# The edge stage of a four-layer graph network: a fixed order for ScalarE's copies and one-hots

## The chip, the cores and the metric

One core of one Trainium2 chip. The metric is the device time of one execution in microseconds; the median of three timed runs is shown. Besides it there is one profiled execution, whose trace gives every instruction's start and duration.

Names used below: TensorE (PE, matrix multiply; its weight loads are PEld), VectorE (DVE), ScalarE (ACT), GpSimd (POOL) and SyncE (SP, which here only issues transfers). Each engine runs its own instructions in a fixed order that is laid out when the program is built; between engines they wait for one another by semaphores. SBUF is the on-chip memory, PSUM the accumulator memory that TensorE writes, divided into banks.

## The reference, cut to what matters

Four graph layers over 3125 nodes of 128 features and 103125 edges, which are sorted by their target `dst`; each layer is followed by a residual addition and a layer norm. The stage in question works for all four: it turns the list of edges into dense matrices. The first layer is

```python
def _L0_gnn_ref(x, edge_row, edge_col, edge_val, weight, b):
    xw = x @ weight
    msgs = edge_val[:, None] * xw[edge_col]
    out = jax.ops.segment_sum(msgs, edge_row, num_segments=N_NODES)
    return jax.nn.relu(out + b)
...
edge_index = jnp.stack([src, dst])
x = _layernorm(x + _L0_gnn_ref(x, src, dst, edge_weight, L0_gnn_weight, L0_gnn_b), axis=-1)
x = _layernorm(x + _L1_gnn_ref(x, edge_index, ...), axis=-1)
x = _layernorm(x + _L2_gnn_ref(x, ...), axis=-1)
x = _layernorm(x + _L3_gnn_ref(x, edge_index, ...), axis=-1)
```

(with the weights' names shortened). The second and third layers are attentions over the same edges, the fourth takes means over them twice. The kernel replaces the gathers and segment sums by products with two dense 3125 x 3125 matrices: how often an edge from one node to another occurs (the counts), and the sum of those edges' weights (the weights). As several edges can share a pair of nodes, both are sums.

## The kernel before, in words

**The matrices.** The edge stage makes both matrices from one-hot vectors. A *window* takes five nodes (`WN` = 5) and up to 256 edge slots, which lie as two halves of 128 on the partitions. An edge's source node is written as a row d (0 to 127) within a block c (0 to 24). `ohd` holds, for each edge slot, the one-hot of d; `ohc` the one-hot of the pair (node of the window, block c), 125 of 128 columns (`KW` = 125). A product of the two over the edge slots gives the counts of a window. For the weights `ohd` is multiplied by the edge's weight first; to keep single precision, the weight is split into three bfloat16 parts, and so there are three such tensors, `wod[0]`, `wod[1]` and `wod[2]`.

**Batches and groups.** Sixteen windows (`BW` = 16) form a batch, four windows a group; there are 40 batches (`NBT`), the last with one group, 157 groups in all. For each batch `make(b)` (from line 827) has VectorE make `ohd` and `ohc` (line 849) and the `wod` (line 860): the first two for both halves, the third for the first half only. The second half of the third is made by ScalarE, window by window: `more(k)` (line 863) is four activations that scale one window's one-hot each (line 866). These sixteen per batch are the *one-hots on ScalarE* of this text. The pools `f_oh` (two buffers for each of `ohd`, `ohc`) and `f_of` (six for the `wod`) hold two batches, so the tensors of batch b+1 are made while TensorE works on batch b.

**One group.** For group k of batch b TensorE adds eight matmuls (line 893: four windows, two halves) into the bank `cp`, the counts, and 24 (line 901: four windows, two halves, three parts) into the bank `wp`, the weights. ScalarE then casts `cp` into `cs` in bfloat16 (line 906) and copies `wp` into `ws` (line 912). `cp` and `wp` come from one pool of three PSUM banks (`f_cps`, tag "cw"); the transposes for new keys (lines 675 and 676) use the same three. In the program's text, the four one-hots of the next batch's group k stand between the cast of `cs` and the copy of `ws` (lines 906 to 912).

**After a batch.** SyncE stores `ws` into the dense matrix `wd` (line 914) and, after every second batch, `cs` into the matrix of counts `ctd` (line 917). In the first two batches `xw_of` multiplies the features by the first layer's weights (lines 760 to 770). From the third batch on `add0` (line 801) begins the first layer's sum: for 128 finished rows of `wd` it loads two tiles `cw` of ten blocks each (line 807) and adds them into five banks that stay open, by fp32 matmuls (line 811); the trace counts 40 of them for 128 rows. Every eighth batch `keys_of` (lines 659 to 699) prepares the keys and weights of the next 128 windows, with six transposes on TensorE and copies on VectorE and ScalarE.

**What sets the order.** The text of the program gives each instruction its rank; the tool that builds the program goes through the engines with its own estimates of time and lets the first-ranked ready instruction of each engine go next. The order so found is fixed: on the chip each engine takes its instructions in it. `tc.issue_after(i)` adds an edge of order without a semaphore: what is traced inside stands after instruction i on i's engine. Before the change none is used for these copies and one-hots, so a one-hot may be put ahead of copies of its own and earlier groups as soon as `ohd` of its batch is made.

Of the kernel before, what the change touches and what calls it, by code (L numbers as in the profile page):

```python
# [10 lines left out]
AF = mybir.ActivationFunctionType  # L11
# [6 lines left out]
NB = 25  # L18
# [471 lines left out]
WN = 5  # L490
NW = 640
NG = 5
BW = 16
KW = WN * NB
# [16 lines left out]
def fast_path(  # L511
# [4 lines left out]
    nc = tc.nc  # L516
# [225 lines left out]
    def products_of_weights():  # L742
        nc.gpsimd.tensor_tensor(both, gb_row, sb_row, OP.add)
        tw = {}
        for name, w in (("l1", l1_wt), ("q", wqt), ("k", wkt), ("v", wvt)):
            t = zps.tile([P, P], F32, name="trw", tag="acc3")
            nc.tensor.transpose(t, w, ident)
            tw[name] = ep.tile([P, P], F32, name="tw_" + name)
            nc.scalar.copy(tw[name], t)
        t = zps.tile([P, P], F32, name="trw", tag="acc3")  # L750
        nc.tensor.matmul(t[:, 0 : 2 * H], tw["l1"], att, start=True, stop=True)
        nc.scalar.copy(watt, t[:, 0 : 2 * H])
        t = zps.tile([P, P], F32, name="trw", tag="acc3")
        nc.tensor.matmul(t, tw["q"], tw["k"], start=True, stop=True)
        nc.scalar.copy(wyv[:, 0:P], t)
        t = zps.tile([P, P], F32, name="trw", tag="acc3")
        nc.tensor.matmul(t, tw["v"], wot, start=True, stop=True)
        nc.scalar.copy(wyv[:, P:], t)

    def xw_of(b0, n):  # L760

        t = zps.tile([P, 512], F32, name="trx", tag="acc0")
        for k in range(n):
            nc.tensor.transpose(t[:, k * P : (k + 1) * P], x[:, b0 + k, :], ident)
        xT = ep.tile([P, 512], F32, name="f_xTb", bufs=2)
        nc.scalar.copy(xT[:, : n * P], t[:, : n * P])
        t = zps.tile([P, 512], F32, name="trx", tag="acc2")
        for k in range(n):
            nc.tensor.matmul(t[:, k * P : (k + 1) * P], xT[:, k * P : (k + 1) * P], l0_wt, start=True, stop=True)
        nc.scalar.copy(xw[:, b0 : b0 + n, :].rearrange("p b d -> p (b d)"), t[:, : n * P])  # L770
# [26 lines left out]
    def bias0(acc, n):  # L797
        for j in range(n):
            nc.tensor.matmul(acc[:, j, :], ones, l0_br, start=(j == 0), stop=False, skip_group_check=True)

    def add0(pool, i, accs, blocks):

        b0, n = blocks
        for h in range(0, n, 10):
            m = min(10, n - h)
            cw = pool.tile([P, min(10, n), P], F32, name="cw")[:, 0:m]
            nc.sync.dma_start(
                cw.rearrange("p c d -> p (c d)"), wd[i * P : (i + 1) * P, (b0 + h) * P : (b0 + h + m) * P]
            )
            for j in range(h, h + m):  # L810
                nc.tensor.matmul(  # L811
                    accs[j // 4][:, j % 4, :], cw[:, j - h, :], xw[:, i, :], start=False,
                    stop=(i == NB - 1 and (j % 4 == 3 or j == n - 1)), skip_group_check=True,
                )
# [12 lines left out]
    def make(b):  # L827

        if b % 8 == 2 and 8 < b < NBT - 8:
            keys[b // 8 + 1] = keys_of(b // 8 + 1)  # L830
        kd2, kc2, w2, w3 = keys[b // 8]
        ohd = op_.tile([P, 2 * BW, P], BF16, name="ohd")
        ohc = op_.tile([P, 2 * BW, P], BF16, name="ohc")

        def twos(k):
            k = k[:, b % 8, :, :, :].rearrange("p q w t -> p (q w) t")
            return k[:, :, None, :].to_broadcast([P, 2 * BW, P // 2, 2])

        def some(s):
            if b < NBT - 1:  # L840
                return [slice(0, 2 * BW if s < 2 else BW)]
            return [slice(0, LW)] + ([slice(BW, BW + LW)] if s < 2 else [])

        def packed(o, ww):
            return o[:, ww].rearrange("p w (a t) -> p w a t", t=2)

        for o, k in ((ohd, kd2), (ohc, kc2)):
            for ww in some(0):
                nc.vector.tensor_tensor(  # L849
                    packed(o, ww), twos(k)[:, ww],  # L850
                    ramp.rearrange("p (a t) -> p a t", t=2)[:, None, :, :].to_broadcast(
                        [P, ww.stop - ww.start, P // 2, 2]
                    ),
                    OP.is_equal,
                )
        wod = []
        for s in range(3):
            f = of_.tile([P, 2 * BW, P], BF16, name="wod")
            for ww in some(s):
                tip[s] = nc.vector.tensor_tensor(packed(f, ww), packed(ohd, ww), twos(w2[s])[:, ww], OP.mult)  # L860
            wod.append(f)

        def more(k):
            for w in range(k, k + 4):
                at = (b % 8) * BW + w
                nc.scalar.activation(wod[2][:, BW + w, :], ohd[:, BW + w, :], AF.Copy, scale=w3[:, 1, at : at + 1])  # L866

        return ohd, ohc, wod, more

    cs = None  # L870
    acc0 = None
    done = 0
    cur = make(0)
    with tc.issue_after(tip[0].ins), tc.issue_after(tip["keys"].ins):
        keys[1] = keys_of(1)
# [2 lines left out]
    for b in range(NBT):  # L878
        ohd, ohc, wod, _ = cur
        cur = make(b + 1) if b + 1 < NBT else None  # L880
        nw = BW if b < NBT - 1 else LW
        if b % SB == 0:
            cs = sp.tile([P, NB, SB * BW * WN], BF16, name="cs")
            if b + SB == NBT:
                nc.gpsimd.memset(cs[:, :, ((SB - 1) * BW + LW) * WN :], 0.0)
        ws = sp.tile([P, BW, P], F32, name="ws")
        for k in range(0, nw, 4):
            cp = cps.tile([P, 4, P], F32, name="cp", tag="cw")
            wp = cps.tile([P, 4, P], F32, name="wp", tag="cw")
            for j in range(4):  # L890
                for q in range(2):
                    w = q * BW + k + j
                    nc.tensor.matmul(  # L893
                        cp[:, j, 0:KW], ohd[:, w, :], ohc[:, w, 0:KW], start=(j == 0 and q == 0), stop=(j == 3 and q == 1),
                        skip_group_check=True,
                    )
            for j in range(4):
                for q in range(2):
                    w = q * BW + k + j
                    for s in range(3):  # L900
                        made = nc.tensor.matmul(  # L901
                            wp[:, j, :], ohc[:, w, :], wod[s][:, w, :], start=(j == 0 and q == 0 and s == 0),
                            stop=(j == 3 and q == 1 and s == 2), skip_group_check=True,
                        )
            i0 = (b % SB) * BW * WN + k * WN
            nc.scalar.copy(  # L906
                cs[:, :, i0 : i0 + 4 * WN].rearrange("p c (w i) -> p c w i", i=WN),
                cp[:, :, 0:KW].rearrange("p w (i c) -> p c w i", c=NB),
            )
            if cur and (b + 1 < NBT - 1 or k < LW):  # L910
                cur[3](k)
            nc.scalar.copy(ws[:, k : k + 4, :], wp)  # L912
        for a, e in ((0, 112), (112, KW)):
            nc.sync.dma_start(wv_[b * BW : b * BW + nw, a:e, :].rearrange("w k d -> k w d"), ws[a:e, 0:nw, :])
        if b % SB == SB - 1:
            i0 = (b - SB + 1) * BW * WN
            nc.sync.dma_start(ctd[:, :, i0 : i0 + SB * BW * WN].rearrange("c d i -> d c i"), cs)
        if b < 2:
            for blocks in GB[4 * b : 4 * b + 4]:
                xw_of(*blocks)  # L920
        if b == 2:
            with tc.issue_after(made.ins):
                products_of_weights()
            acc0 = [zps.tile([P, 4, P], F32, name=f"acc{k}", tag=f"acc{k}") for k in range(Z0 // 4)]
            for a in acc0:
                bias0(a, 4)
        while acc0 and (done + 1) * P <= (b - 1) * BW * WN:
            add0(zp, done, acc0, (0, Z0))
            done += 1
# [150 lines left out]
    with ExitStack() as st:  # L1080
# [119 lines left out]
        cp = st.enter_context(tc.tile_pool(name="f_cp1", bufs=6))  # L1200
# [120 lines left out]
        for x_, (g, hp, c) in enumerate(items):  # L1321
            i0, n = IG[g]
# [49 lines left out]
    scale = float(P) ** -0.5  # L1372
    with ExitStack() as st:
        l2 = st.enter_context(tc.tile_pool(name="f_lp2", bufs=1))
        yT = l2.tile([P, NP], F32, name="yT")
        cp = st.enter_context(tc.tile_pool(name="f_cp2", bufs=3))
# [79 lines left out]
        for x_, (q, c) in enumerate(items):  # L1456
            i0, n = QG[q]
# [40 lines left out]
    with ExitStack() as st:  # L1498
        fp = st.enter_context(tc.tile_pool(name="f_fp3", bufs=1))
        cp = st.enter_context(tc.tile_pool(name="f_cp3", bufs=HB + 1))  # L1500
# [77 lines left out]
        for k in range(K + 3):  # L1578
            if k < K:
                for b in range(NB - HB, NB):  # L1580
                    add1(last[b], b, k)
                c, n = CN[k]
# [172 lines left out]
```

## Time and profile before

| what | value |
|---|---|
| median of three timed runs | 1514.52 us (1514.36 to 1517.14) |
| the profiled execution: time | 1519.3 us |
| its span, first to last instruction | 1517.5 us |
| busy share of PE / PEld / DVE / ACT over the span | 92% / 80% / 65% / 60% |
| mean granted TensorE clock | 0.983 |
| first cast of `cs`, end of the last copy of `ws` | 47.2 us, 469.2 us |

The costliest rows of the edge stage by the page's list of groups:

| line, engine | what | times | mean ns of one | busy us |
|---|---|---|---|---|
| 901 PE | wp, 24 per group | 3768 | 219 | 239.1 |
| 893 PE | cp, 8 per group | 1256 | 218 | 95.7 |
| 811 PE | first layer's sum | 1000 | 278 | 118.7 |
| 860 DVE | wod | 122 | 1870 | 221.2 |
| 866 ACT | one-hots | 628 | 399 | 192.8 |
| 912 ACT | copy of ws | 157 | 584 | 91.7 |

The mean of a matmul is its whole passage; matmuls overlap, so a group's busy time is far below count times mean, and the pace of TensorE is read from starts. The same holds for ScalarE and VectorE to a lesser degree (a one-hot of 395 ns follows another after some 295 ns). In the timeline a line gives start, duration, engine, line, and in brackets the idle time before it and what ended it; "x12" means that twelve instructions of one kind stood in a row. Of the 1000 matmuls of line 811, 160 belong to rows and blocks that are done after the edge stage.

### The profile page before, as it was taken

The page shows a single profiled execution, that of the slowest core. Times are in us where ns is not written, and L with a number is a line of the kernel's source. Part 1 is how long each engine was busy: PE and PEld are TensorE (multiplying, and loading weights), DVE is VectorE, ACT ScalarE, POOL GpSimd, SP SyncE. Part 2 cuts the span into 40 slices and gives each one's busy share as a digit, 9 for nine tenths or more (in the row PEclk, how much of TensorE's full clock was granted, in tenths as well). Part 3 has the DMA queues.
Part 4 walks back from the last instruction along what each step waited for, and adds up shares of the span by engine and source line. Part 5 has one row for each costly group of instructions (what it writes and reads, how often), then busy time and mean ns, then how long its engine had stood idle before and what let it go on. Part 6 is the DMA issues. An engine that isn't in the chain of part 4 may idle for free.

```text
span 1517.5 us, 35041 instructions
## 1 busy us (share of the span) xinstructions
PE 1390.6 (92%) x14775; PEld 1218.8 (80%) x14775; DVE 982.5 (65%) x1621; ACT 906.6 (60%) x1847; POOL 129.5 (9%) x164
## 2 busy tenths in 40 slices
PE   4898999999998988988979989899999999999995
PEld 3898999899897888987978979677777774458995
DVE  4999998989991389887898879534465352012006
ACT  2988888878882479877867788454555331023003
POOL 1000000000000022231132113200000000000000
PEclk9999999999999999999999999999999999999998
DMA  7368787877889644443433434332222218513541
GB/s 204 92 177 235 209 225 188 242 197 210 234 225 261 200 131 119 112 130 112 135 95 105 143 89 116 117 118 73 69 60 80 73 59 303 195 44 130 197 154 46
DMA packets 209734, 223.92 MB, mean 148 GB/s; under 512 B 72988, under 2 KB 183371, under 8 KB 209309
## 3 DMA queue, kind: packets, MB, share of 16 engines
q1 hardware_dynamic: 208780, 218.51, 49.6%
q8 instruction: 117, 1.92, 0.5%
q0 software_dynamic: 400, 1.97, 0.4%
q10 hardware_dynamic: 385, 1.11, 0.2%
q14 instruction: 52, 0.43, 0.1%
HBM read 157.19 MB, written 64.36 MB: 146 GB/s over the span
## 4 chain that ended last, share of the span: by engine, by line
PE 71%; ACT 12%; DVE 9%; DMA 3%; issue 3%; POOL 2%; SPq 0%; ACTq 0%; DVEq 0%; POOLq 0%
PE acc L1272 9%; PE acc L1423 9%; PE wp L901 8%; PE s L1415 8%; PE acc L811 7%; PE acc L1523 7%; PE acc L1599 6%; ACT wod L866 5%; PE acc L1267 5%; DVE cm L1257 3%; PE cp L893 3%; PE left L811 2%; ACT ws L912 2%; DMA cw<-wd 1%; DVE cm L1250 1%
## 5 line engine op out<-in xcount | busy, mean ns | idle before, releaser
L1272 PE MATMUL acc<-vp,cm 128*128 128x198 bf16 x2500 | 343.4, 251 | 7.6 <-DVE cm L1257 6.6
L1267 PE MATMUL acc<-vp,ct 128*128 128x204 bf16 x1250 | 317.0, 255 | 9.7 <-DVE vp L1175 4.5
L1256 ACT ACTIVATE fm<-adr,bas 128x768 bf16<-128x768 f32 (+1 forms) x320 | 287.1, 952 | 62.3 <-DVE cm L1257 60.5
L1272 PEld LDWEIGHTS <-cm 128*128 128x128 bf16 x2500 | 235.8, 98 | 24.5 <-DVE cm L1257 8.9
L901 PE MATMUL wp<-wod,ohc 128*128 128x128 bf16 x3768 | 239.1, 219 | 5.6 <-ACT cs L906 5.6
L901 PEld LDWEIGHTS <-ohc 128*128 128x128 bf16 x3768 | 219.9, 98 | 6.7 <-issue 6.3
L860 DVE TENSOR_TENSOR wod<-ohd,w 128x4096 bf16<-128x4096 bf16 (+2 forms) x122 | 221.2, 1870 | 0.6 <-PE wp L901 0.6
L1257 DVE TENSOR_TENSOR cm<-fm,ct 128x768 bf16<-128x768 bf16 (+1 forms) x320 | 200.5, 658 | 32.2 <-PE acc L1272 17.3
L866 ACT ACTIVATE wod<-ohd,wu 128x128 bf16<-128x128 bf16 x628 | 192.8, 399 | 0.0
L1419 DVE TENSOR_TENSOR e<-e,ct 128x416 f32<-128x416 f32 (+1 forms) x175 | 108.1, 624 | 110.3 <-ACT e L1418 102.6
L1418 ACT ACTIVATE e<-s,f_nm 128x416 f32<-128x416 f32 (+1 forms) x175 | 109.5, 632 | 103.1 <-PE s L1415 95.8
L1423 PEld LDWEIGHTS acc<-self__8020,e 128*128 128x128 f32 x1250 | 148.2, 192 | 19.8 <-issue 18.9
L1423 PE MATMUL acc<-self__8020,e 128*128 128x129 f32 x1250 | 148.5, 276 | 0.0
L1415 PE MATMUL s<-yT,f_xT 128*128 128x416 f32 (+1 forms) x350 | 143.1, 544 | 4.5 <-ACT rt L1395 2.5
L1267 PEld LDWEIGHTS <-ct 128*128 128x128 bf16 x1250 | 122.1, 98 | 3.9 <-issue 2.7
L811 PE MATMUL acc<-f_xw,cw 128*128 128x128 f32 x1000 | 118.7, 278 | 6.1 <-DMA cw<-wd 6.1
L811 PEld LDWEIGHTS acc<-f_xw,cw 128*128 128x128 f32 x1000 | 115.1, 194 | 6.7 <-DMA cw<-wd 6.7
L912 ACT COPY ws<-wp 128x512 f32<-128x512 f32 x157 | 91.7, 584 | 48.1 <-PE wp L901 47.0
L893 PE MATMUL cp<-ohc,ohd 128*128 128x125 bf16 x1256 | 95.7, 218 | 23.4 <-ACT ws L912 19.4
L1415 PEld LDWEIGHTS s<-yT,f_xT 128*128 128x128 f32 x350 | 62.5, 192 | 55.3 <-issue 40.8
L849 DVE TENSOR_TENSOR ohd<-kd,ramp 128x4096 bf16<-128x4096 bf16 (+1 forms) x41 | 90.1, 2199 | 23.5 <-PE cp L893 23.5
L893 PEld LDWEIGHTS <-ohd 128*128 128x128 bf16 x1256 | 78.3, 98 | 28.7 <-issue 28.6
(319 smaller groups left out, 1535.3 us busy)
## 6 DMA issues: line engine op xcount, KB each, us to landing
ct<-f_ctd SPq DMA_DIRECT2D x46, 800.0 KB
wd<-ws SPq DMA_DIRECT2D x39, 896.0 KB
cw<-wd SPq DMA_DIRECT2D x50, 640.0 KB
ct<-f_ctd SPq DMA_DIRECT2D x150, 192.0 KB
f_ctd<-cs SPq DMA_DIRECT2D x20, 1000.0 KB
ct<-f_ctd SPq DMA_DIRECT2D x50, 224.0 KB
ct<-f_ctd SPq DMA_DIRECT2D x25, 416.0 KB
ct<-f_ctd SPq DMA_DIRECT2D x25, 365.2 KB
```

The source lines that it names most:

```text
L811: nc.tensor.matmul(accs[j // 4][:, j % 4, :], cw[:, j - h, :], xw[:, i, :], start=False, stop=(i == NB - 1 and (j % 4 == 3 or j == n - 1)) ...
L860: tip[s] = nc.vector.tensor_tensor(packed(f, ww), packed(ohd, ww), twos(w2[s])[:, ww], OP.mult)
L866: nc.scalar.activation(wod[2][:, BW + w, :], ohd[:, BW + w, :], AF.Copy, scale=w3[:, 1, at : at + 1])
L893: nc.tensor.matmul(cp[:, j, 0:KW], ohd[:, w, :], ohc[:, w, 0:KW], start=(j == 0 and q == 0), stop=(j == 3 and q == 1), skip_group_check=True,)
L901: made = nc.tensor.matmul(wp[:, j, :], ohc[:, w, :], wod[s][:, w, :], start=(j == 0 and q == 0 and s == 0), stop=(j == 3 and q == 1 and s ...
L912: nc.scalar.copy(ws[:, k : k + 4, :], wp)
L1256: nc.scalar.activation(f[:, : n * P], at, AF.Relu, bias=bas[:, c, h : h + 1], scale=UP)
L1257: nc.vector.tensor_tensor(m[:, : n * P], f[:, : n * P], ct[:, : n * P], OP.min)
L1267: nc.tensor.matmul(out_(F1, PW), ct[:, k * P : (k + 1) * P], vp[:, c, hp : hp + 2, :, 2 * F1 : V1], start=(c == 0), stop=False, skip_group ...
L1272: nc.tensor.matmul(out_(0, 2 * F1)[:, j], ms[j][:, k * P : (k + 1) * P], vp[:, c, hp + j, :, 0 : 2 * F1], start=False, stop=(c == NB - 1 a ...
L1415: nc.tensor.matmul(s[:, :m], xT[:, c * P : (c + 1) * P], yT[:, i0 * P + a : i0 * P + a + m], start=True, stop=True)
L1423: nc.tensor.matmul(acc[k // 3][:, (k % 3) * (P + 1) : (k % 3 + 1) * (P + 1)], es[q, c][:, k * P : (k + 1) * P], vo[:, c, 0 : P + 1], start ...
```

## The change

ScalarE's order within a group is fixed by edges: first the cast of `cs`, then the copy of `ws`, then the four one-hots of the next batch, and only then the cast of the next group. The instructions and their operands are the same.

```diff
         def more(k):
             for w in range(k, k + 4):
                 at = (b % 8) * BW + w
-                nc.scalar.activation(wod[2][:, BW + w, :], ohd[:, BW + w, :], AF.Copy, scale=w3[:, 1, at : at + 1])
+                made = nc.scalar.activation(wod[2][:, BW + w, :], ohd[:, BW + w, :], AF.Copy, scale=w3[:, 1, at : at + 1])
+            return made
...
     done = 0
+    ahead = []
     cur = make(0)
...
             i0 = (b % SB) * BW * WN + k * WN
-            nc.scalar.copy(
-                cs[:, :, i0 : i0 + 4 * WN].rearrange("p c (w i) -> p c w i", i=WN),
-                cp[:, :, 0:KW].rearrange("p w (i c) -> p c w i", c=NB),
-            )
+            with ExitStack() as q_:
+                if ahead:
+                    q_.enter_context(tc.issue_after(ahead[-1].ins))
+                nc.scalar.copy(
+                    cs[:, :, i0 : i0 + 4 * WN].rearrange("p c (w i) -> p c w i", i=WN),
+                    cp[:, :, 0:KW].rearrange("p w (i c) -> p c w i", c=NB),
+                )
+            copied = nc.scalar.copy(ws[:, k : k + 4, :], wp)
             if cur and (b + 1 < NBT - 1 or k < LW):
-                cur[3](k)
-            nc.scalar.copy(ws[:, k : k + 4, :], wp)
+
+                with tc.issue_after(copied.ins):
+                    ahead.append(cur[3](k))
```

The edge stands on the cast of `cs` (after the last one-hot made so far) and on the one-hots (after the copy of `ws` of their group); the copy of `ws` itself has no edge, but needs its group's matmuls. The sixteen one-hots of batch 0, made ahead of the loop, are not touched.

## The prediction

> **What bounds the kernel now.** I read the 40 slices of the page first: TensorE (PE) and VectorE (DVE) are both at eight or nine tenths from slice 1 to slice 11, which is the edge stage (42 to 469 us), and ScalarE (ACT) is just below them. The change touches only this stage, so I went to its stretches. The starts of VectorE's ohd repeat to the hundredth every eight batches (140.21, 228.48, 316.75), so two such periods were asked for:
>
> ```profile
> core 0: us, PE busy (x) PEld busy (x) DVE busy (x) ACT busy (x) POOL busy (x), PEclk, DMA share, GB/s
> 140.21:228.48 88.27, 81.84 (x1234) 80.64 (x1231) 82.10 (x50) 72.81 (x202) 0.00 (x0) 1.00 0.80 215
> 228.48:316.75 88.27, 81.84 (x1234) 80.64 (x1231) 81.63 (x47) 72.52 (x201) 0.00 (x0) 1.00 0.80 216
> ```
>
> Eight batches take 88.27 us. VectorE works 81.6 to 82.1 of them, TensorE 81.8, ScalarE 72.5 to 72.8, at full clock. None is full: three queues in fixed order wait for one another. The view of waits for 60 to 460 us says where:
>
> ```profile
> ACT ws L912 <- PE wp L901: 44.3, 65, 1.4
> ...
> DVE ohd L849 <- PE cp L893: 23.5, 18, 1.7
> PE cp L893 <- ACT ws L912: 18.8, 16, 1.6
> ACT cs L906 <- PE cp L893: 14.6, 16, 2.5
> ```
>
> TensorE waits 16 times, 18.8 us in all, for a copy of ws to free a bank of the accumulator; VectorE waits 23.5 us for TensorE to be done with an old one-hot buffer; ScalarE waits often and short. The 23.5 us are the most that any new order on ScalarE can win, since VectorE's own work stays. The timeline of 200 to 222 us shows what lies around these waits:
>
> ```profile
> 201.77 3.62 ACT L866 ACTIVATE wod<-ohd,wu 128x128 bf16<-128x128 bf16 x12
> ...
> 205.28 0.57 ACT L912 COPY ws<-wp 128x512 f32<-128x512 f32 x1
> 205.75 0.57 ACT L906 CAST cs<-cp 128x500 bf16<-128x500 f32 x1
> 205.90 0.60 PE L893 MATMUL cp<-ohc,ohd 128*128 128x125 bf16 x8 [1.56 <-ACT ws L912]
> ...
> 206.22 1.28 ACT L866 ACTIVATE wod<-ohd,wu 128x128 bf16<-128x128 bf16 x4
> ...
> 207.40 0.57 ACT L912 COPY ws<-wp 128x512 f32<-128x512 f32 x1
> ...
> 210.98 4.79 ACT L866 ACTIVATE wod<-ohd,wu 128x128 bf16<-128x128 bf16 x16
> ...
> 211.50 4.68 PE L811 MATMUL acc<-f_xw,cw 128*128 128x128 f32 x40
> ...
> 216.33 0.58 ACT L912 COPY ws<-wp 128x512 f32<-128x512 f32 x1 [0.56 <-PE wp L901]
> ```
>
> Two things are to be seen. At 201.77 ScalarE makes twelve one-hots in a row, the copy of ws stands behind them, and TensorE idles 1.56 us. But at 210.98 it makes sixteen in a row while TensorE is in a chunk of 40 matmuls of line 811 and needs nothing copied: there the row of one-hots costs nothing, and ScalarE idles only 0.56 us after it.
>
> **What the change does to the queue.** No instruction is added or removed: 157 casts of cs, 157 copies of ws and 628 one-hots remain. The two kinds of ordering edge fix ScalarE's order as cs(g), ws(g), four one-hots, cs(g+1), ws(g+1), four one-hots. So two things change: no copy stands behind twelve one-hots any more, and no one-hot can be made ahead of the copies of its own group. The second adds a wait: behind the copy of ws, which waits for the group's 24 matmuls of line 901, now stand four one-hots, and behind them the next cast, whose bank TensorE needs for the group after.
>
> **One group in the new order.** From the rows above, ws to cs is 0.47 us (205.28 to 205.75), cs to the first one-hot 0.47, four one-hots 1.18 (206.22 to 207.40): 2.12 us for a group whatever the order. TensorE's group is shorter: in the chain of waits eight matmuls of line 893 take 0.44 and 24 of line 901 1.34, together 1.78. So without anything else ScalarE sets the pace. How far ahead can TensorE be? The pool has three banks, taken in turn, so the wp of a group needs the bank that the cast of the group before gave back. Count from the start of ws(g): the one-hots end their turn at 1.65, cs(g+1) runs 1.65 to 2.23, wp(g+2) then 2.27 to 3.61, and its last result is there at about 3.77 (the 24 matmuls last 1.50 in the timeline, 0.16 beyond their 1.34). ScalarE wants it for ws(g+2) at 4.24. TensorE is thus 0.47 us ahead, no more.
>
> **What a chunk of line 811 then costs.** A period has 200 matmuls of line 811, five chunks of 40, 4.52 us each in the chain. Where a chunk falls inside a wp (most of them do now), ws comes 4.52 - 0.47 = 4.05 us late and ScalarE has nothing that it is allowed to do. Where it falls between wp(g+1) and cp(g+2), it runs from 1.48 to 6.00, cp(g+2) is there at 6.60, wp(g+2) at 7.95, so ws(g+2) starts at 7.98 instead of 4.24: 3.74 late. Five chunks cost 18.7 to 20.3 us of ScalarE's time in each period; I take 3.9 each, 19.5, nearer to the inner place.
>
> **The sum of a period.** ScalarE's work 72.5, the chunks 19.5, and its wait in the making of new keys: before it idles 1.63 us there, for VectorE; in the new order it comes to that place later, so between 0 and 1.63, taken as 0.4. Sum 92.4 against 88.27, +4.1 (ends 91.2 and 94.4, +2.9 and +6.1). VectorE (82.1) and TensorE (81.8) lie below, so ScalarE and TensorE in turn are the chain. The removed waits of TensorE (18.8 in 400 us, 4.1 in a period) are already in this sum: they go, and about 8 us of new waits for line 811 come.
>
> **How many periods.** Chunks of 40 stand in the queue from 123.4 to 459.6 us, 336 us or 3.8 periods: 3.8 x 4.1 = +15.6 us. Before 123 there are two chunks of 20 only, and VectorE is busy 50.00 us of the stretch 60 to 110: it sets the pace there and hides them; taken as nothing, at most 2 x (2.26 - 0.47) = 3.6 if that cover were gone, and no gain, as VectorE is full. After 469 us nothing changes but the start. **Copies and transfers:** the copy of ws now comes ahead of its batch's last one-hots, so the stores of lines 914 and 917 on SyncE's queue can only be issued a little earlier within the batch; the loads of line 807 stand behind them, and no wait of TensorE for a load is seen before 469 us, so both are costed at nothing; the cover is the many us between the issue of a load (203.04) and its chunk (211.50). Were it gone, a chunk would come later, at the same price. The one-hots of a batch need VectorE's ohd, which is 2.3 us of work begun when the last cp of the batch before the current one is done; the first of them is due only 0.44 + 2 x 1.34 + 0.47 us after that at the earliest, so they wait for nothing, or some 0.3 us where VectorE is itself the later one.
>
> The profiled execution is 1519.3 us with a span of 1517.5; the median of the timed runs is 1514.5. The difference of +15.6 is put on the median: 1530.
>
> The Trainium skill, "Perfetto Trace Analysis", section Optimizing Scalar/DVE Operations, says that where ScalarE is not saturated but makes bubbles on other engines, its work should be broken up so that something can be done sooner. That speaks for this change, and the 1.56 us row is such a bubble; by the rule alone all 18.8 us would go, and the time would be about 1496. The row at 210.98 is why I don't follow it: the long rows of one-hots also fill ScalarE's own holes.
>
> **Rivals.** *Chunks absorbed, faster.* TensorE waits 2.12 - 1.78 = 0.34 us in each group of the new order, 10.9 in a period. If its queue, which the same ordering pass lays out anew, puts the matmuls of line 811 into these waits, only 22.6 - 10.9 = 11.7 stay uncovered: 72.5 + 11.7 + 0.4 = 84.6, -3.7 in a period, -14 in all: 1500. It decides from the point where more than 7.2 us of line 811 are hidden in a period (88.27 - 72.5 - 0.4 = 15.4 may stay open). For it: single matmuls of line 811 can go between any two others. Against it: all twenty chunks after 123 us are whole, and they stand at places where TensorE was not waiting.
>
> *Halves apart, no change.* A chunk is two halves of 20, from two loads. Apart, and between groups, a half costs 1.48 (the sum of the second place with 2.26): 10 x 1.48 + 72.5 = 87.3, with 0 to 1.63 for the keys 87.3 to 88.9, so -3.7 to +2.5 us in all: about 1514. For it: the first two rows of blocks (89.9 and 103.8 us) went so. Against it: none later.
>
> *The order does not change.* If the copies were laid out as now the time stays 1514.5. Against it: the edges leave no freedom but for ws to come earlier.
>
> **Chances and range.** Forecast 0.73, with its own range 1525 to 1541 (+11 from 91.2; +23 from 94.4, and the 3.6 of the first part); chunks absorbed 0.13; halves apart 0.12, a quarter of it beyond the bound to either side taken to faster; no new order 0.02. A measurement of this kernel tells 0.2% (3 us) from no change. That makes slower 0.73, same 0.11, faster 0.16. The range reaches down to half of the absorbed case and up to near the end of the forecast's own: 1508 to 1540.
>
> **What would show it.** Right: on ScalarE four one-hots at a time and never twelve; the wait of cp for ws gone from 18.8 to near nothing; ScalarE waiting about 4 us for wp in each chunk of line 811; the period 92 us; VectorE's wait for cp grown from 23.5 to some 35 to 40 us; the stage's last ws at about 485 instead of 469. Wrong: chunks of line 811 split to fewer than 20 matmuls, waits of ws below 3 us a chunk, or a period bound by VectorE at 82 to 85 us.

## The result, and the profile after

The changed kernel takes 1537.99 us (median of six runs), the kernel before beside it 1520.02 us; the ratio is 1.0118 with a 95% interval of 1.0098 to 1.0138. It is slower by 18 us. The forecast was 15.6 us slower.

The loss lies in the edge stage alone. From the first cast of `cs` to the end of the last copy of `ws` it takes 441.1 us instead of 422.0; what follows takes 1047.2 instead of 1048.3. The page's rows of busy time are as before (VectorE 982.6 us, ScalarE 903.0 instead of 906.6), so no work was added; engines wait longer. Two periods of eight batches, each from 0.4 us ahead of a start of VectorE's ohd (busy time of each engine in each stretch):

```profile
core 0: us, PE busy (x) PEld busy (x) DVE busy (x) ACT busy (x) POOL busy (x), PEclk, DMA share, GB/s
258.24:349.01 90.77, 85.64 (x1234) 82.67 (x1232) 81.77 (x46) 71.87 (x201) 0.00 (x0) 0.98 0.80 210
349.01:439.50 90.49, 84.10 (x1228) 80.65 (x1226) 80.05 (x40) 69.00 (x193) 0.00 (x0) 1.00 0.79 210
```

A period of 90.8 and 90.5 us stands where 88.27 stood, with VectorE and ScalarE no busier; TensorE shows 2 to 4 us more for no more matmuls. The loss is not even: the eight batches before these two take 86.5 us (from the start of ohd at 172.16 to that at 258.63). The view of waits for 60 to 480 us (who waited for whom, us in total, times, longest) says which waits grew:

```profile
ACT ws L915 <- PE wp L903: 54.0, 39, 4.0
...
DVE ohd L849 <- PE cp L895: 32.6, 19, 3.0
ACT ws L915 <- issue: 22.3, 6, 4.0
PE wp L903 <- ACT cs L911: 20.6, 61, 1.9
ACT cs L911 <- PE cp L895: 8.3, 7, 2.6
```

TensorE's 16 waits of cp for ws (18.8 us) are gone from the list. In their place ScalarE's copy of ws waits 76 us in two rows instead of 44, with a longest wait of 4.0 instead of 1.4, and TensorE's wp waits 61 times for a cast (20.6 us instead of 4.2): TensorE waits for ScalarE about as long as before, at another place. The timelines of ScalarE and of TensorE, 88 to 122 us, show two such places:

```profile
90.33 1.30 ACT L866 ACTIVATE wod<-ohd,wu 128x128 bf16<-128x128 bf16 x4
91.51 0.58 ACT L911 CAST cs<-cp 128x500 bf16<-128x500 f32 x1
96.12 0.59 ACT L915 COPY ws<-wp 128x512 f32<-128x512 f32 x1 [4.03 <-issue]
96.60 1.28 ACT L866 ACTIVATE wod<-ohd,wu 128x128 bf16<-128x128 bf16 x4
...
104.57 0.61 ACT L915 COPY ws<-wp 128x512 f32<-128x512 f32 x1
106.28 0.59 ACT L915 COPY ws<-wp 128x512 f32<-128x512 f32 x1 [1.10 <-PE wp L903]
106.76 1.27 ACT L866 ACTIVATE wod<-ohd,wu 128x128 bf16<-128x128 bf16 x4
```

```profile
90.02 1.39 PE L903 MATMUL wp<-wod,ohc 128*128 128x128 bf16 x22 [0.18 <-ACT cs L911]
91.24 4.68 PE L811 MATMUL acc<-f_xw,cw 128*128 128x128 f32 x40
...
110.19 1.50 PE L903 MATMUL wp<-wod,ohc 128*128 128x128 bf16 x24 [1.04 <-ACT cs L911]
```

At 91.24 TensorE turns to a chunk of line 811 with two matmuls of a wp still to come. ScalarE has cast `cs` and stands before the copy of that wp for 4.03 us, the next one-hots behind it; before the change it made sixteen one-hots in such a hole. (The profile names "issue" where it finds no semaphore; the wp whose end the copy needs is on TensorE's timeline.) At 106.28 a second thing is seen: two copies of ws in a row, with 1.10 us of idle between. The copy has no edge, and the tool that laid out the queue let it overtake the first one-hots of a new batch; TensorE's wp at 110.19 then waits 1.04 us for a cast that comes late.

### The profile page after: what moved, and what is told of

It is laid out like the page before. It is cut to its first block, busy times and chain, and to the rows that moved or that the text cites. A ratio compares the mean times of both kernels' runs of the same rounds, so it can differ in the third digit from the quotient of the medians.

```text
span 1535.7 us, 35038 instructions
## 1 busy us (share of the span) xinstructions
PE 1403.7 (91%) x14762; PEld 1223.2 (80%) x14775; DVE 982.6 (64%) x1621; ACT 903.0 (59%) x1847; POOL 130.0 (8%) x164
## 4 chain that ended last, share of the span: by engine, by line
PE 63%; ACT 18%; DVE 9%; issue 4%; DMA 3%; POOL 2%; SPq 0%; DVEq 0%; ACTq 0%; POOLq 0%
PE acc L1430 9%; PE acc L1279 9%; PE s L1422 8%; ACT wod L866 8%; PE wp L903 6%; PE acc L1530 6%; PE acc L1606 6%; PE acc L811 5%; PE acc L1274 4%; ACT cs L911 3%; DVE cm L1264 3%; ACT ws L915 3%; PE left L811 2%; ACT fm L1263 1%; DVE cm L1257 1%
## 5 line engine op out<-in xcount | busy, mean ns | idle before, releaser
L903 PEld LDWEIGHTS <-ohc 128*128 128x128 bf16 x3768 | 224.6, 98 | 43.4 <-issue 42.7
L866 ACT ACTIVATE wod<-ohd,wu 128x128 bf16<-128x128 bf16 x628 | 201.4, 400 | 0.0
L1274 PEld LDWEIGHTS <-ct 128*128 128x128 bf16 x1250 | 122.3, 98 | 4.0 <-issue 2.7
L849 DVE TENSOR_TENSOR ohd<-kd,ramp 128x4096 bf16<-128x4096 bf16 (+1 forms) x41 | 90.1, 2200 | 37.5 <-PE cp L895 32.6
L1606 PEld LDWEIGHTS <-ct 128*128 128x128 bf16 x1725 | 96.9, 98 | 0.0
```

The lines of the kernel that those rows point to most:

```text
L866: made = nc.scalar.activation(wod[2][:, BW + w, :], ohd[:, BW + w, :], AF.Copy, scale=w3[:, 1, at : at + 1])
L903: made = nc.tensor.matmul(wp[:, j, :], ohc[:, w, :], wod[s][:, w, :], start=(j == 0 and q == 0 and s == 0), stop=(j == 3 and q == 1 and s ...
L1274: nc.tensor.matmul(out_(F1, PW), ct[:, k * P : (k + 1) * P], vp[:, c, hp : hp + 2, :, 2 * F1 : V1], start=(c == 0), stop=False, skip_group ...
L1606: nc.tensor.matmul(acc[g][:, j, :], ct[:, (b0 + j) * P : (b0 + j + 1) * P], ups[b // 4][:, b % 4, s, :], start=(b == 0 and s == 0 and j == ...
```

## The experiments

Ten kernels were run. "Stage" is the time from the first cast of `cs` to the end of the last copy of `ws` in the profiled execution, 422.0 us before and 441.1 after; ratios are to the kernel before on the same chip.

| run | order on ScalarE | line 811 in the stage | stage, us | ratio (95%) |
|---|---|---|---|---|
| before | free | 22 pieces, 20 of them of 40 | 422.0 | 1 |
| after | both edges | 32 pieces, 14 of 40 | 441.1 | 1.0118 (1.0098 to 1.0138) |
| oh_edge | one-hots behind ws | 23 pieces, 19 of 40 | 433.2 | 1.0086 (1.0066 to 1.0105) |
| cs_edge | cast behind one-hots | 28 pieces | 430.9 | 1.0042 (1.0029 to 1.0055) |
| d_before | free | as filler, 260 matmuls | 395.4 | 1.0303 (1.0280 to 1.0326) |
| d_after | both edges | as filler, 382 matmuls | 398.8 | 1.0215 (1.0193 to 1.0238) |
| wholes | both edges | 20 chunks of 40 | 444.5 | 1.0147 (1.0125 to 1.0168) |
| halves | both edges | 43 chunks of 20 | 435.6 | 1.0056 (1.0032 to 1.0080) |
| eighths | both edges | 115 chunks of 8 or 4 | 405.7 | 0.9875 (0.9853 to 0.9896) |
| eighths_free | free | 115 chunks of 8 or 4 | 418.5 | 0.9948 (0.9928 to 0.9968) |
| strict | three edges | 31 pieces | 434.7 | 1.0060 (1.0042 to 1.0079) |
| eighths_strict | three edges | 115 chunks of 8 or 4 | 405.1 | 0.9857 (0.9832 to 0.9882) |

**Line 811 taken out of the stage, in both orders.** The loop that starts it after each batch is dropped; all 25 rows of blocks are added by the loop that follows the stage.

```diff
-        while acc0 and (done + 1) * P <= (b - 1) * BW * WN:
-            add0(zp, done, acc0, (0, Z0))
-            done += 1
     for i in range(done, NB):
         add0(zp, i, acc0, (0, Z0))
```

> The order of before, with the sum of the first layer (line 811) and its loads taken out of the edge stage: all 25 rows of blocks follow it. The whole time grows, since 840 matmuls of 0.113 us (95 us) and their loads lie behind the stage; only the edge stage (first to last copy of ws, 419 us before) and the comparison with d_after count. Theory A (the loss comes from the chunks of line 811, during which the new order leaves ScalarE with nothing that it may do): stage 385 to 405 us here. Rival B (the fixed order costs by itself, through the three banks and its pace of 2.12 us a group): the same here, as this run has no fixed order.

> The order of after, with line 811 and its loads taken out of the edge stage in the same way. Theory A: without chunks the fixed order loses nothing; the stage is as long as that of d_before or up to 12 us shorter (VectorE sets the pace, 82 to 84 us for eight batches, 380 to 395 us in all). Rival B: the stage is 10 to 19 us longer than that of d_before, as it is in after against before.

The edit did not do quite what it says: having the lowest rank now, line 811 was laid out as a filler wherever TensorE would have waited, in pieces of 2 to 10 or 12 matmuls, 260 of them in d_before's stage and 382 in d_after's. That is as good a test, since no chunk of 40 is left. The stages are 395.4 and 398.8 us: the fixed order costs 3.4 us where it cost 19.1 with the chunks, and 122 more matmuls of line 811 (13.8 us at 0.113) lie inside it; as a whole d_after is the faster of the two, 1554.2 against 1565.9 us. So the loss comes from the chunks and the order together, not from the order alone; rival B (10 to 19 us) falls, though 3.4 lies just above the range that I gave theory A. (The 3.4 us hold a cost of another kind too: in d_after a copy of ws overtakes one-hots 19 times, as at 106.28 above, with 23.0 us of idle before the second copy.)

**One edge alone.** In oh_edge the cast has no edge, in cs_edge the one-hots have none.

```diff
# oh_edge
-                if ahead:
-                    q_.enter_context(tc.issue_after(ahead[-1].ins))
# cs_edge
-                with tc.issue_after(copied.ins):
-                    ahead.append(cur[3](k))
+                ahead.append(cur[3](k))
```

> Only the edge that holds the one-hots behind the copy of ws of their group; the cast of the next group is free of the one-hots. Theory A: this edge carries the loss, ratio to before 1.007 to 1.016, ScalarE still waits some 4 us for wp in a chunk of line 811. Rival D (the loss comes from the cast standing behind the one-hots, which frees TensorE's bank late): ratio 0.990 to 1.003.

> Only the edge that holds the cast of a group behind the one-hots made last; the one-hots are free to be made ahead of the copies of ws. Theory A: ScalarE can fill the chunks with one-hots again, most of the loss goes: ratio 0.992 to 1.005. Rival D: ratio 1.007 to 1.016 here.

Both lie within theory A's ranges, but not as clearly as hoped: the edge on the one-hots costs 11.2 us of stage, the one on the cast 8.9, together about what both cost at once (19.1). Neither is the whole of it, and what the cast's edge costs, and how, stays open. cs_edge has twelve overtaking copies as well, with 13.7 us of idle, and two pieces of 60 matmuls. That the cast frees TensorE's bank late, as rival D says, is not shown: TensorE's wp waits 18.3 us for a cast in cs_edge, but 25.9 us in oh_edge, where the cast has no edge.

**The size of the chunks, the order held fixed.** Line 811 is cut into portions that an edge holds behind the last matmul of a group, seven groups after their load was started; the portion is 20, 10 or 4 calls (40, 20 or 8 matmuls), and for the smallest the tiles `cw` hold five blocks instead of ten, in six buffers instead of three. The form for the smallest:

```diff
+            at_group += 1
+            n0 = 4
+            while n0 and tiles and tiles[0][0] + 7 <= at_group:
+                with tc.issue_after(made.ins):
+                    tiles.pop(0)[1]()
+                n0 -= 1
+            if acc0 and (done + 1) * P <= (b - 1) * BW * WN and len(tiles) <= 25:
+                load0()
             i0 = (b % SB) * BW * WN + k * WN
...
-        while acc0 and (done + 1) * P <= (b - 1) * BW * WN:
-            add0(zp, done, acc0, (0, Z0))
-            done += 1
```

Here `load0` loads one tile and appends its matmuls to `tiles`; `made` is the group's last matmul.

> The fixed order of after, with the matmuls of line 811 put in chunks of 20 between two groups (tiles of ten blocks, as now; 43 chunks in the stage, none longer). Theory A: a chunk costs ScalarE 1.48 us instead of 4 for 40, so a period of eight batches comes to 72.5 + 10 x 1.48 + 0.4 = 87.7 us, near that of before (88.27); ratio to before 0.997 to 1.006. Rival B (the fixed order costs by itself): ratio 1.009 to 1.015, as in after.

> The fixed order of after, with line 811 in 20 whole chunks of 40 between groups, none split; beside halves it settles what a whole chunk costs. Theory A: 3.74 us each where a half costs 1.48, so the stage is 20 x 3.74 - 43 x 1.48 = 11 us longer than that of halves (435.6), 444 to 450 us; ratio 1.010 to 1.018. Rival E (size does not matter, VectorE's or the start's losses decide): stage within 4 us of halves, ratio 1.003 to 1.008.

> The fixed order of after, with line 811 in chunks of 8 matmuls (four calls, 0.9 us; tiles of five blocks) between two groups, 115 chunks in the stage. Theory A: TensorE's group is 1.78 + 0.71 = 2.49 us on average, 79.6 us in a period, most of it in the wait that ScalarE's 2.12 us leaves; VectorE (82 us) sets the pace; a period 82 to 85 us, the stage 395 to 408 us, ratio 0.983 to 0.993, faster than both kernels. Rival B: ratio 1.003 to 1.015.

From wholes to halves to eighths the stage goes 444.5, 435.6, 405.7 us, with the same edges throughout (from batch 12 to 28 eight batches take 91.8, 89.9 to 90.6 and 83.26 us), though the stage of wholes holds the fewest matmuls of line 811 (800; halves 860, eighths 852). The three ratios lie in theory A's ranges: the fixed order is slow with large chunks and fast with small ones. ScalarE's order is not quite the same in the three, since a copy of ws overtakes one-hots 21, 10 and 1 times, with 23.2, 11.0 and 1.1 us of idle; the pair strict and eighths_strict below is free of that. ScalarE's timeline in wholes, at a chunk between two groups that TensorE runs from 163.30 to 167.8:

```profile
165.56 1.29 ACT L866 ACTIVATE wod<-ohd,wu 128x128 bf16<-128x128 bf16 x4
168.46 0.58 ACT L936 CAST cs<-cp 128x500 bf16<-128x500 f32 x1 [1.60 <-PE cp L912]
169.80 0.59 ACT L940 COPY ws<-wp 128x512 f32<-128x512 f32 x1 [0.76 <-PE wp L920]
```

The cast waits for a cp that comes after the chunk, and then the copy for a wp that comes after the cp; in halves the same pair of waits is 0.53 and 0.76 us, 1.29 together, at 270.46 and 271.80 (0.92 and 0.76 where one half follows another after a single group). Behind chunks of 8 the cast waits for nothing and the copy some 0.5 us:

```profile
271.30 0.56 ACT L936 CAST cs<-cp 128x500 bf16<-128x500 f32 x1
272.32 0.59 ACT L940 COPY ws<-wp 128x512 f32<-128x512 f32 x1 [0.47 <-PE wp L920]
272.80 1.28 ACT L866 ACTIVATE wod<-ohd,wu 128x128 bf16<-128x128 bf16 x4
```

and the stretches of two periods of eighths show what sets the pace then:

```profile
core 0: us, PE busy (x) PEld busy (x) DVE busy (x) ACT busy (x) POOL busy (x), PEclk, DMA share, GB/s
162.19:245.45 83.26, 81.87 (x1234) 81.20 (x1231) 81.53 (x46) 72.78 (x201) 0.00 (x0) 1.00 0.88 229
245.45:328.71 83.26, 81.87 (x1234) 81.20 (x1232) 81.54 (x46) 72.79 (x201) 0.00 (x0) 1.00 0.88 229
```

The same busy times as before the change, in 83.26 us instead of 88.27; VectorE and TensorE are nearly full.

> As eighths, but with ScalarE's order of before (no edges), so that long rows of one-hots stay, now with no chunk to lie in. Theory A: the rows of 12 hold up a copy and with it TensorE (1.56 us each time), so this is slower than eighths: a period 84 to 88 us, ratio 0.988 to 1.000. Rival B: without the fixed order it is faster than eighths by 10 us or more.

eighths_free tells whether the small chunks alone do it. They give 0.9948; the fixed order on top gives 0.9875. So with small chunks the change is worth some 11 us, as theory A has it, but by another way than I wrote: four rows of twelve one-hots are left there, of 17 before. The view of waits for 60 to 460 us says what holds it up:

```profile
ACT cs L931 <- PE cp L910: 55.7, 38, 2.2
...
DVE ohd L849 <- PE cp L910: 11.7, 11, 2.7
```

ScalarE waits 38 times for a cp: 28 times its queue has the casts of two groups in a row (11 times before the change), the second too early, with the copy of the first group's wp behind it.

**The overtaking copy.** One edge more puts the copy of ws behind the one-hots made last, in after (strict) and in eighths (eighths_strict).

```diff
-            copied = nc.scalar.copy(ws[:, k : k + 4, :], wp)
+            with ExitStack() as q_:
+                if ahead:
+                    q_.enter_context(tc.issue_after(ahead[-1].ins))
+                copied = nc.scalar.copy(ws[:, k : k + 4, :], wp)
```

> After, with one edge more: the copy of ws too stands behind the one-hots made last, so that it can't overtake the first one-hots of a batch as it does in after (cast, copy, a wait of 1.10 us, copy, one-hots). Theory F: the overtaking is a cost, each one 1.1 us on ScalarE and 1.04 us on TensorE, some 14 times; without it the stage is 5 to 15 us shorter than that of after, ratio 1.002 to 1.009. Rival G: ScalarE then waits for VectorE's ohd at the start of a batch instead, or another engine sets the pace there: stage within 4 us of after, ratio 1.009 to 1.015.

> The same edge added to eighths, for the best version. Theory F: 0.980 to 0.987, a little faster than eighths (0.9875), bounded by VectorE's 82 us a period. Rival G: the same as eighths within 0.2%.

After has 15 overtakings with 16.5 us of idle between the two copies, strict has none, and its stage is 6.4 us shorter (434.7). So some 6 us of the loss of after are no part of what the change says it does, but of one edge that it lacks; why not the whole 16.5 was not tried. One reason shows in wholes: where an overtaking stands close before a chunk (161.33 before 163.30), the cast waits 1.55 to 1.60 us at the chunk, elsewhere 2.75 to 2.85; the one-hots put off fill part of the hole. The pieces of line 811 differ too (strict has 12 of 40 and 17 of 20, after 14 and 12), so this is not the edge in pure form. In eighths there was one overtaking, and eighths_strict can't be told from eighths: stages of 405.1 and 405.7 us, overlapping intervals of the ratio. Eighths is faster than the kernel before beside it by 18 us, eighths_strict by 22.

Strict and eighths_strict are the cleanest pair: ScalarE's queue in the stage is the same in both, instruction by instruction, and no copy overtakes. Only line 811 differs: pieces of up to 40 matmuls in strict, of 8 or 4 in eighths_strict, with its smaller tiles. The stages are 434.7 and 405.1 us, where the free order has 422.0 (before) and 418.5 (eighths_free). So one and the same order of ScalarE loses 12.7 us with large pieces and wins 13.4 with small ones. Not tried was the free order with whole chunks at the places of wholes.

## Why the prediction was right

**The sign and the mechanism hold.** ScalarE's order is cast, copy, four one-hots: 152 rows of four in the trace and none of twelve. The wait of cp for ws went, as forecast. The price of a chunk inside a wp was forecast as 4.05 us of idle ScalarE; eight of the fourteen whole chunks in after show 3.99 to 4.04, the other six 2.3 to 2.8. A chunk between groups was put at 3.74 and a half at 1.48; in wholes the cast waits 45.8 us in 19 times, 2.4 each, and the copy 0.76 after it, 3.2 together (at the place shown 2.36), and halves show 1.29 to 1.68. The last ws ends at 488.5 us (forecast 485). VectorE's wait for cp grew from 23.5 to 32.6 us where 35 to 40 were forecast (with 4.8 for a cast and 4.2 for wp its waits are 41.6 us in all). Two of the signs of being wrong came in part: five pieces of line 811 have fewer than 20 matmuls, and six whole chunks cost less than 3 us.

**The total is right by two sizes that were off in opposite directions; that is luck in part.** The lateness against before at the first copy of ws of a batch, counted from the first cast. The second row is an estimate: it takes off the matmuls of line 811 that are merely done earlier than before, at 0.113 us each (4.52 us for 40).

| batch | 4 | 6 | 10 | 12 | 20 | 28 | 36 | 38 | last |
|---|---|---|---|---|---|---|---|---|---|
| after, us late | 5.9 | 8.2 | 12.6 | 11.5 | 8.7 | 11.2 | 14.6 | 16.0 | 19.1 |
| after, less early work | 1.5 | 3.7 | 5.9 | 7.0 | 8.1 | 11.2 | 14.6 | 16.0 | 16.9 |
| wholes | 1.8 | 3.8 | 5.8 | 4.6 | 10.5 | 12.0 | 15.6 | 16.8 | 22.5 |
| halves | 1.8 | 3.4 | 5.4 | 4.1 | 5.8 | 8.1 | 9.4 | 10.1 | 13.6 |
| eighths | 1.8 | 2.6 | -0.9 | -2.8 | -7.8 | -12.8 | -18.1 | -18.6 | -16.3 |

*The first part was put at nothing, at most 3.6 us.* Behind 180 matmuls of line 811, where before had 120, batch 10 comes 12.6 us late; less the 6.8 us of early work that is 5.9, of which 1.7 to 1.8 come in the first batches whatever the chunks. The forecast had some 1.5 at this point ((155.0 - 123.4) / 88.27 x 4.1, batch 10 being at 155.0 us before). The term that was off is "it sets the pace there and hides them". In the new queue three whole chunks of 40 stand at 91.2, 113.4 and 135.5 us, where before there were two halves and then wholes from 123 on, and each shows a wait of 4.03 us on ScalarE. VectorE, which had no idle time from 60 to 110 us, then idles 2.83, 2.31 and 2.31 us (from 97.6, 120.4 and 142.7): an engine that is always busy hides a delay only so far as it has worked ahead, and here that was 1.2 to 1.7 of the four microseconds. The first of the three, in VectorE's timeline:

```profile
100.43 2.29 DVE L849 TENSOR_TENSOR ohd<-kd,ramp 128x4096 bf16<-128x4096 bf16 x1 [2.83 <-PE cp L895]
```

*The steady rate was put at +4.1 us for eight batches; after shows +1.0, or +2.5 less early work.* From batch 12 to 36, three periods, the lateness grows from 11.5 to 14.6, less early work from 7.0 to 14.6. The term that was off is "five chunks, 3.9 each" (19.5 us). Between these two marks there are nine wholes, behind which ScalarE waits 28.5 us (3.2 each), nine halves with 11.8 us (0.6 to 2.1 each), and shreds: 13.4 us a period. The rival "halves apart" was thus mixed into the forecast case, where I had kept the two asunder. The overtakings, which the prediction saw as possible ("for ws to come earlier") and did not price, work against this: eleven, 4.0 us a period. Where no chunk is split, in wholes, the same three periods give 4.6 to 15.6, +3.7 a period. That this lies near +4.1 is no proof of the sum: 560 matmuls lie between the marks there and 600 before, a chunk costs 3.2 us and not 3.74, and overtakings add what the sum has not.

*The rivals.* Chunks absorbed (1500 us) did not come by itself, but eighths is that case made on purpose: a period of 83.26 us (forecast for it 84.6), ratio 0.9875, which times the median shown of before is 1495.6 us. Halves apart was forecast at no change and came to 1.0056 when made: a period of 89.9 to 90.6, not 87.3 to 88.9. What I left out there is VectorE, which in halves waits 18.0 us for casts (13 times), the second half of a pair, which costs 1.68 and not 1.48, and ten overtakings (11.0 us); what each is worth was not tried. (The two halves at 89.9 and 103.8 us that spoke for this rival are one row of blocks, not two.)

The Trainium skill ("Perfetto Trace Analysis", Optimizing Scalar/DVE Operations) says of ScalarE and VectorE that where they are not saturated but cause bubbles on other engines, "breaking up instructions may allow work to be completed sooner". Here no instruction was broken up, only rows of them. That went both ways: by itself it cost 1.2%, and with the large pieces on TensorE broken up too, it was worth 0.7% (0.9948 to 0.9875).

## What to carry to other kernels

When two engines feed each other through a few banks, a long row of independent work on one of them may be what fills the hole that a long row on the other makes. Look at both rows before you break up one. Here breaking up the other, TensorE's chunks of 4.5 us, took the stage from 434.7 to 405.1 us with ScalarE's queue unchanged, and made a gain of the fixed order.

An edge of order fixes only what it names: what has no edge is still placed by the tool's estimate, and may take the gap.

## What the runs showed of the hardware that was not expected

In the profile of after the granted clock of TensorE drops within the edge stage: 0.86 and 0.89 in the stretches 325 to 332 and 332 to 339 us, against 1.00 throughout both periods shown of before and of eighths. It follows a wait of TensorE of 1.85 us for a cast, and the row behind that wait takes 2.36 us for 24 matmuls instead of 1.50:

```profile
327.21 0.60 PE L895 MATMUL cp<-ohc,ohd 128*128 128x125 bf16 x8
329.66 2.36 PE L903 MATMUL wp<-wod,ohc 128*128 128x128 bf16 x24 [1.85 <-ACT cs L911]
331.81 1.04 PE L895 MATMUL cp<-ohc,ohd 128*128 128x125 bf16 x8
332.65 1.91 PE L903 MATMUL wp<-wod,ohc 128*128 128x128 bf16 x24
```

The two wp and the cp take 1.7 us longer there ((2.36 - 1.50) + (1.04 - 0.60) + (1.91 - 1.50)), a small part of the 19.1. Another wait of that length was not followed by it (1.85 us before the wp at 240.13 in the same trace), so what sets it off stays open; it was not tried.
